# Key sums of a two-layer graph attention kernel: VectorE transposes in place of one TensorE matmul a visit, with the inverses made ahead

## The chip, the cores and the metric

One core of one Trainium2 chip runs the whole program. The metric is the device time in microseconds (us) of one execution, as the median of several. All input, weights and output are float32 in the device's memory; the adjacency is one byte per pair.

## The reference

There are 64 graphs of 256 nodes with 512 features. Two layers follow each other, each of them "normalise the row, clip below zero, attend over the graph's neighbours, add to the input". Layer 0 has 4 heads of 64, layer 1 has 8 heads of 64 with one more normalisation inside and the diagonal always allowed.

```python
h = jnp.maximum(_layernorm(x, axis=-1), 0.0)
x = x + _L0_gnn_ref(h, adj, Wq, Wk, Wv, Wo, bo)
h = jnp.maximum(_layernorm(x, axis=-1), 0.0)
x = x + _L1_gnn_ref(h, adj, gamma, beta, w_qkv, w_out, b_out)
# one attention layer, in short
q, k, v = split_heads(h @ Wq), split_heads(h @ Wk), split_heads(h @ Wv)
sim = jnp.where(mask, einsum('bhid,bhjd->bhij', q, k) * scale, neg)
out = einsum('bhij,bhjd->bhid', softmax(sim, axis=-1), v)
return merge_heads(out) @ Wo + bo
```

The change concerns the softmax's denominator: for every head and query, the sum over the 256 keys of the exponentials, and its inverse, with which the attention's output is multiplied.

## The kernel before

**Tiles and steps.** Two graphs make one step, so there are 32 steps. A step's rows are 4 tiles of 128 nodes by 512 features. Queries, keys and values come from seven matmul products of half-size blocks in place of eight, so a stage such as "project queries and keys" is seven products one after the other (the order `SET`), each of which fills one of four PSUM banks (`mm_tile`, which goes round the four and skips held ones). Two of the seven products are added on to the bank of an earlier one: product 2 goes on to the bank of product 1, and so cannot start until product 1's bank was copied out. In the value projection of layer 1 (`project_v1`, matmuls at L857) it is ScalarE that copies product 1 out, at L750.

**Scores are transposed.** `scores` (L933) leaves keys on the partitions and queries in the free dimension. VectorE adds the mask (L956), ScalarE takes the exponentials in place (L961), GpSimd adds the two key halves (`key_halves`, L968, into `pd`). VectorE transposes `pd` in blocks of 32x32 and sums each block's rows (`turn_keys` L974 and `key_quarters` L981). What is then left, in `part`, is 128 partitions by 32 for each pair of heads: four partition groups of 32, a part of the keys in each. The sum over these four groups is the denominator.

**A visit.** A visit ends one pair of heads' attention and starts another's: `key_sums` of the earlier unit, its weighted values (`weigh_out`, L1004 and the copy L1016), then the scores of the next unit. `key_sums` adds the four groups with one matmul against a 0/1 matrix `quarters` (L1032), inverts (L1036), takes a running maximum for a guard (L1037), writes the inverses to a line in device memory (L1043) and reads each line back, the same for 64 partitions (four DMAs at L1047). `normalise` (L1063, GpSimd) multiplies the attention's output with it. There are 97 calls of `key_sums`: three a step and a few at the edges.

**The order.** The work of every step is a list of events with places, made by hand: `at(period, place, fn)`. A period is 6.4 places long, and in the steady part each holds: `combine` of layer 1 of the step before (place 1.0), a visit at `AT_X` (2.0) with the value projection of layer 1 behind it, `combine` of layer 0 (3.0), queries and keys of layer 1 (3.5), a visit at `AT_Q0` (4.5) with queries and keys of layer 0, values of layer 0 (5.5), a visit at `AT_Z` (6.2). TensorE, VectorE, ScalarE and GpSimd keep the order of this list. SyncE, which issues most DMAs, does not: the build orders its DMAs by when it expects each to be ready, and the order is then fixed in the program.

**DMAs around the visit at `AT_X`.** Here the finished rows of a step leave (`store_graph`, L907, once for each of the two graphs, on SyncE), the inverses are read (L1047), the blocks of the next layer's transposed input are moved with 16 DMAs (`move_blocks`, L711, on SyncE), and the rows of the step after next are read into the buffer that the stores have emptied (`load_graph`, L505, twice, on ScalarE's queue). The two loads stand in ScalarE's own order of instructions, directly ahead of the exponentials of the visit.

```python
at(p, AT_X + 0.005 if s > 1 else 1.2, load_graph, s, 1)
at(p, AT_X + 0.025 if s > 1 else 1.2, load_graph, s, 0)
...
at(p, place + 6 / 7 + 0.001, store_graph, s, 1)
at(p, place + 1.05, store_graph, s, 0)
```

Of the kernel before, what the change touches and what calls it, by code (L numbers as in the profile page):

```python
# [8 lines left out]
FP = mybir.dt.float32  # L9
# [4 lines left out]
ALU = mybir.AluOpType  # L14
# [301 lines left out]
def fast_path(  # L316
# [19 lines left out]
    nc = tc.nc  # L336
    P = 128
# [3 lines left out]
    NSTEP = B // G  # L341
    NIC = N // P
    NT = G * NIC
    T = G * N
# [6 lines left out]
    const = ctx.enter_context(tc.tile_pool(name="const", bufs=1))  # L351
    io = ctx.enter_context(tc.tile_pool(name="io", bufs=2))
    act = ctx.enter_context(tc.tile_pool(name="act", bufs=1))
    sm = ctx.enter_context(tc.tile_pool(name="sm", bufs=2))
    stat = ctx.enter_context(tc.tile_pool(name="stat", bufs=4))
    dram = ctx.enter_context(tc.tile_pool(name="dram", bufs=2, space=bass.MemoryType.DRAM))
# [5 lines left out]
    banks, held = ["m0", "m1", "m2", "m3"], set()  # L362

    def mm_tile(shape, dt=FP, hold=False):
        tag = next(b for b in banks if b not in held)
        banks.remove(tag)
        banks.append(tag)
        if hold:
            held.add(tag)
        return ps_mm.tile(shape, dt, name="mm", tag=tag)  # L370
# [6 lines left out]
        nc.vector.tensor_scalar(offdiag[:, g, :], ident, -1.0, 1.0, op0=ALU.mult, op1=ALU.add)  # L377
    onesb = const.tile([P, P], BF, name="onesb")
    nc.vector.memset(onesb, 1.0)
    quarters = const.tile([P, 32], FP, name="quarters")  # L380
    nc.vector.tensor_tensor(quarters, ident[:, 0:32], ident[:, 32:64], ALU.add)
    for k in (2, 3):
        nc.vector.tensor_tensor(quarters, quarters, ident[:, 32 * k:32 * (k + 1)], ALU.add)
    nc.vector.memset(extremes, 0.0)
    mhalf = const.tile([P, NT], FP, name="mhalf")
    nc.gpsimd.memset(mhalf, -0.5)
# [38 lines left out]
    wqkv1 = const.tile([P, NB, HC, 3, H1], FP, name="wqkv1")  # L425
# [51 lines left out]
    S = [dict() for _ in range(NSTEP)]  # L477
# [433 lines left out]

    units, sums_bank = [0], []

    def scores(s, lyr, pr, second):
        st = S[s]
        qk = st.pop(("qk", lyr, pr))

        sc = [  # L920
            [mm_tile([P, NIC, N]) if second and g == 0 else ps_sc.tile([P, NIC, N], FP, name="sc") for e in range(2)]
            for g in range(G)
        ]
        if second and sums_bank:
            tag = sums_bank.pop()
            banks.remove(tag)
            banks.append(tag)
        for g in range(G):
            for kc in range(NIC):
                for e in range(2):  # L930
                    rows = slice(e * DH, (e + 1) * DH)
                    k0 = g * N + kc * P
                    nc.tensor.matmul(  # L933
                        sc[g][e][:, kc, :], qk[rows, 1, k0:k0 + P],
                        qk[rows, 0, g * N:(g + 1) * N], start=True, stop=True,
                    )

        last = (s, lyr) == (NSTEP - 1, 1)
        if last and pr == 1:
            both = act.tile([P, 2, G, NIC, N], FP, name="p", tag="h")  # L940
            p = [both[:, e] for e in range(2)]
        elif last and pr == 3:
            p = [
                wqk0[:, 4:6].rearrange("p n c k o -> p (n c k o)").rearrange("p (g k n) -> p g k n", g=G, k=NIC),
                act.tile([P, G, NIC, N], FP, name="p", tag="v0"),
            ]
        else:
            p = [sm.tile([P, G, NIC, N], FP, name="p", bufs=4) for _ in range(2)]
        st["sc", lyr, pr], st["p", lyr, pr] = sc, p
# [74 lines left out]
    def key_sums(s, lyr, prs):  # L1024

        st = S[s]
        part = st.pop(("part", lyr, prs))
        rows = 32 * len(prs)
        bank = mm_tile([P, 32])
        sums_bank[:] = [banks[-1]] if len(prs) > 1 else []  # L1030
        sums = bank[:rows]
        nc.tensor.matmul(  # L1032
            sums, part[:, :len(prs)].rearrange("p i b -> p (i b)"), quarters, start=True, stop=True
        )
        inv = stat.tile([P, 32], FP, name="inv", bufs=1)[:rows]
        nc.vector.reciprocal(inv, sums)  # L1036
        nc.vector.tensor_tensor_reduce(  # L1037
            out=sums, in0=sums, in1=inv, scale=1.0, scalar=0.0, op0=ALU.add, op1=ALU.max,
            accum_out=extremes[:rows, units[0]:units[0] + 1],
        )  # L1040
        units[0] += 1
        line = dram.tile([len(prs), 2, T], FP, name="line")
        nc.sync.dma_start(line.rearrange("i e (b q) -> (i e b) q", q=32), inv)  # L1043
        for i, pr in enumerate(prs):
            invb = inverse_place(s, lyr, pr, i if len(prs) > 1 else pr % 2)
            for e in range(2):
                nc.sync.dma_start(  # L1047
                    invb[e * DH:(e + 1) * DH].rearrange("p g n -> p (g n)"),
                    bass.AP(tensor=line.tensor, offset=line[i, e, 0:1].offset, ap=[[0, DH], [1, T]]),
                )  # L1050
            st["invb", lyr, pr] = invb
# [17 lines left out]
    PERIOD, FIRST = 6.4, 6.2  # L1069
# [3 lines left out]
    def at(period, place, fn, *args):  # L1073
        events.append((period * (PERIOD if period >= 0 else FIRST) + place, len(events), fn, args))
# [15 lines left out]
    def visit(period, w, prev, cur):  # L1090

        w -= 0.0003
        s, lyr, prs = prev
        last = (s, lyr) == (NSTEP - 1, 1)
        if prs:
            if prs[0] == 0 and not last:
                at(period, w - 0.0002, place_values, s, lyr)
            at(period, w - 0.0001, key_sums, s, lyr, prs)
            for i, pr in enumerate(prs):
                if not last:  # L1100
                    at(period, w, weigh_out, s, lyr, pr)
                    at(period, w + (0.55 if len(prs) == 1 else (0.3, 0.75)[i]), normalise, s, lyr, pr)
        z, q = w > AT_Z - 0.01 and period < NSTEP - 2, abs(w - AT_Q0) < 0.01 and 0 <= period < NSTEP - 2
        for i, pr in enumerate(cur[2]):
            unit = (*cur[:2], pr)
            one = cur[:2] == (0, 0)
            at(period, w, scores, *unit, i == 1)
            at(period, w, mask_scores, *unit, 0)
            at(period, w + 1 / 7 if one else w, mask_scores, *unit, 1)
            for g, place in enumerate((0.05, 0.22) if one else ((0.02, 0.03), (0.15, 0.3))[i]):  # L1110
                at(period, w + place, exponentials, *unit, g)
            for e, place in enumerate((0.23, 0.3) if one else ((0.1, 0.11), (0.495, 0.496) if z else (0.435, 0.436) if q else (0.35, 0.36))[i]):
                if unit == (1, 0, 1):
                    at(0, 0.45 + place, key_halves, *unit, e)
                else:
                    at(period, w + place, key_halves, *unit, e)
            if cur[:2] == (1, 0):
                period, w, key = 0, 0.0, (*cur[:2], (0, 1), pr)
                turn, add = ((0.44, 0.441), (0.715, 0.87))[pr]
            else:  # L1120
                turn, add = (
                    ((0.31, 0.311), (0.53, 0.531))[pr] if one else ((0.49, 0.491), (0.63, 0.92))[i] if z else
                    ((0.43, 0.431), (1.02, 1.021))[i] if q else ((0.29, 0.291), (0.715, 1.001 if w < AT_X else 0.87))[i]
                )
                key = (*cur, i)
            at(period, w + turn, turn_keys, cur[0])
            at(period, w + add, key_quarters, *key)

    AT_X, AT_C0, AT_QK, AT_Q0, AT_V0, AT_H1, AT_Z = 2.0, 3.0, 3.5, 4.5, 5.5, 6.06, 6.2
# [8 lines left out]
    p = NSTEP - 2  # L1138
# [15 lines left out]
    for s in range(NSTEP):  # L1154

        p = s - 2
# [41 lines left out]
        p = s - 1  # L1198
# [39 lines left out]
        p = s  # L1238
        if s < NSTEP - 1:
# [3 lines left out]
            p, place = (s + 1, 1.0) if s < NSTEP - 2 else (s, LAST_QK + 2)  # L1243
# [5 lines left out]
        else:  # L1249
            p = s - 1  # L1250
# [22 lines left out]
    for i in range(16):  # L1273

        place = (
            *(3.3 - 3.93 + (1 + k) / 7 - 0.0005 for k in range(7)), 0.5205,
            *(0.53 + 0.14 * (k + 1) - 0.0005 for k in range(4)), *(FIRST + 0.9995 for k in range(4)),
        )[i]
        at(-1, place, lambda i=i: weight_block(blocks[i // 4], i // 4, i % 4))
    for i in range(4):  # L1280
        at(-1, 0.1 + 0.01 * i, weight_sum, nc.vector, wqkv1[:, :, :, 0, :], i)
        at(-1, 0.54 + 0.0001 * i, weight_sum, nc.gpsimd, wqkv1[:, :, :, 1, :], i)
        at(0, 0.3, weight_sum, nc.gpsimd, wqkv1[:, :, :, 2, :], i)
        at(0, 1.1, weight_sum, nc.gpsimd, wo1, i)
    for _, _, fn, args in sorted(events, key=lambda e: e[:2]):
        fn(*args)
# [52 lines left out]
```

## Time and profile before

| What | Value |
|---|---|
| Median of 3 runs | 3167.19 us (3165.82 to 3167.96) |
| The profiled execution | 3166.64 us, of which its span is 3164.9 us |
| TensorE (PE) busy | 3136.4 us, 99% of the span |
| GpSimd (POOL) busy | 2237.7 us, 71% |
| VectorE (DVE) busy | 2145.3 us, 68% |
| ScalarE (ACT) busy | 1248.7 us, 39% |
| Mean granted TensorE clock | 0.998 |
| Calls of the key-sum matmul (L1032) | 97, in 194 records |
| SyncE's DMAs of `move_blocks` (L711) | 960 |

A float32 matmul stands in the profile as two records, so the numbers of matmuls in the trace are twice those in the program. Records of TensorE overlap; its pace is read from one start to the next. `SPq` and `ACTq` are the instruction queues of SyncE and ScalarE: a DMA's issue and the wait ahead of it stand there. The arrow behind a gap names what ended it.

### The profile page before, as it was taken

The page shows a single profiled execution, that of the slowest core. Times are in us where ns is not written, and L with a number is a line of the kernel's source. Part 1 is how long each engine was busy: PE and PEld are TensorE (multiplying, and loading weights), DVE is VectorE, ACT ScalarE, POOL GpSimd, SP SyncE. Part 2 cuts the span into 40 slices and gives each one's busy share as a digit, 9 for nine tenths or more (in the row PEclk, how much of TensorE's full clock was granted, in tenths as well). Part 3 has the DMA queues.
Part 4 walks back from the last instruction along what each step waited for, and adds up shares of the span by engine and source line. Part 5 has one row for each costly group of instructions (what it writes and reads, how often), then busy time and mean ns, then how long its engine had stood idle before and what let it go on. Part 6 is the DMA issues. An engine that isn't in the chain of part 4 may idle for free.

```text
span 3164.9 us, 54517 instructions
## 1 busy us (share of the span) xinstructions
PE 3136.4 (99%) x20660; PEld 2582.6 (82%) x20660; DVE 2145.3 (68%) x3590; ACT 1248.7 (39%) x2226; POOL 2237.7 (71%) x2124
## 2 busy tenths in 40 slices
PE   8999999999999999999999999999999999999999
PEld 6788888888888888888888888888888888888887
DVE  6666667666676666666666766667666667666665
ACT  4434444344433444343434434343334434343431
POOL 7776866767767777667677677776776766767753
PEclk9999999999999999999999999999999999999999
DMA  3222222321322322222223223132232222321301
GB/s 127 71 86 71 64 81 70 86 85 51 91 67 78 93 59 74 73 80 86 76 59 90 62 84 87 48 91 70 75 92 64 70 73 79 86 81 52 92 28 48
DMA packets 179851, 237.42 MB, mean 75 GB/s; under 512 B 65272, under 2 KB 69504, under 8 KB 179584
## 3 DMA queue, kind: packets, MB, share of 16 engines
q1 hardware_dynamic: 162832, 202.02, 22.3%
q10 hardware_dynamic: 16752, 31.86, 3.2%
q8 instruction: 165, 2.70, 0.4%
q14 instruction: 102, 0.84, 0.1%
HBM read 136.45 MB, written 34.40 MB: 54 GB/s over the span
## 4 chain that ended last, share of the span: by engine, by line
PE 91%; POOL 3%; DMA 2%; DVE 2%; issue 1%; ACT 0%; SPq 0%; ACTq 0%; POOLq 0%; DVEq 0%
PE mm L816 36%; PE mm L873 17%; PE sc L1004 10%; PE mm L857 10%; PE sc L933 8%; PE mm L843 7%; PE mm L933 2%; DMA out_dram<-xt 1%; POOL xt L511 1%; POOL pd L968 1%; DMA xt<-in_x_dram 1%; PE mm L1032 1%; PE mm L899 0%; POOL oT L1063 0%; DMA h<-in_x_dram 0%
## 5 line engine op out<-in xcount | busy, mean ns | idle before, releaser
L816 PE MATMUL mm<-hT,wqkv 128*128 128x256 f32 x3584 | 787.7, 380 | 0.2 <-DVE qk L756 0.2
L816 PEld LDWEIGHTS mm<-hT,wqkv 128*128 128x128 f32 x3584 | 677.9, 190 | 103.1 <-issue 11.4
L968 POOL TENSOR_TENSOR pd<-p 128x512 f32<-128x512 f32 x383 | 479.4, 1273 | 390.4 <-ACT p L961 250.2
L873 PE MATMUL mm<-wo,oT 128*128 128x256 f32 x2632 | 586.1, 380 | 3.5 <-DVE xt L773 3.2
L873 PEld LDWEIGHTS mm<-wo,oT 128*128 128x128 f32 x2632 | 497.3, 190 | 82.4 <-issue 8.6
L956 DVE TENSOR_TENSOR p<-sc,n 128x512 f32<-128x512 f32 x579 | 363.1, 683 | 271.4 <-PE sc L933 270.0
L961 ACT ACTIVATE p<-p 128x512 f32<-128x512 f32 x766 | 431.8, 624 | 124.7 <-DVE p L956 123.9
L816 PE MATMUL mm<-hT,wqk 128*128 128x256 f32 x1792 | 399.9, 383 | 5.1 <-DVE qk L752 3.7
L857 PE MATMUL mm<-wqkv,hT 128*128 128x256 f32 x1792 | 401.9, 382 | 0.0
L816 PEld LDWEIGHTS mm<-hT,wqk 128*128 128x128 f32 x1792 | 339.0, 191 | 61.5 <-issue 11.8
L857 PEld LDWEIGHTS mm<-wqkv,hT 128*128 128x128 f32 x1792 | 335.5, 190 | 53.4 <-issue 10.3
L1004 PE MATMUL sc<-p,v 128*32 128x256 f32 x6128 | 353.3, 382 | 0.0
L784 POOL TENSOR_TENSOR xt<-xt,u 128x512 f32<-128x512 f32 x183 | 229.9, 1270 | 99.2 <-DVE xt L773 71.6
L933 PE MATMUL sc<-qk 64*128 64x256 f32 x2320 | 292.6, 385 | 0.0
L1004 PEld LDWEIGHTS sc<-p,v 128*32 128x32 f32 x6128 | 190.7, 110 | 119.7 <-issue 2.3
L933 PEld LDWEIGHTS sc<-qk 64*128 64x128 f32 x2320 | 218.7, 186 | 58.4 <-issue 39.2
L974 DVE STREAM_TRANSPOSE turned_p<-pd 128x1024 f32<-128x1024 f32 x192 | 237.1, 1235 | 34.4 <-POOL pd L968 34.4
L1063 POOL TENSOR_TENSOR oT<-oT 128x512 f32<-128x512 f32 x188 | 239.9, 1276 | 3.2 <-DMA oT<-line 3.2
L605 ACT ACTIVATE h<-h,mr,r 128x512 f32<-128x512 f32 x252 | 184.8, 804 | 137.4 <-POOL mr L601 137.4
L981 DVE TENSOR_REDUCE part<-turned_p 128x32 f32<-128x1024 f32 x192 | 233.2, 1215 | 4.4
L843 PE MATMUL mm<-wv,hT 128*128 128x256 f32 x1024 | 227.0, 379 | 0.0
L843 PEld LDWEIGHTS mm<-wv,hT 128*128 128x128 f32 x1024 | 194.2, 190 | 26.7 <-issue 0.3
(141 smaller groups left out, 3738.8 us busy)
## 6 DMA issues: line engine op xcount, KB each, us to landing
h<-blocks SPq DMA_DIRECT2D x960, 64.0 KB, 2.0
oT<-line SPq DMA_DIRECT2D x376, 128.0 KB, 3.3
h<-in_x_dram SPq DMA_DIRECT2D x31, 1024.0 KB, 5.5
out_dram<-xt SPq DMA_DIRECT2D x62, 512.0 KB, 3.6
xt<-in_x_dram ACTq DMA_DIRECT2D x60, 512.0 KB, 5.9
ne<-row SPq DMA_DIRECT2D x30, 256.0 KB, 4.8
ad<-in_adj_dram SPq DMA_DIRECT2D x32, 128.0 KB, 8.5
wr<-in_L_gnn_w_qkv_dram SPq DMA_DIRECT2D x3, 1024.0 KB, 8.9
```

Of the source, the lines that this page charges most:

```text
L816: nc.tensor.matmul(bank[:, k, :], w[:, wa, c, k, a * P:(a + 1) * P], st["hT"][:, ba, c, :], start=first and (k, c) == (0, 0), stop=(k, c) ...
L843: nc.tensor.matmul(bank, st["hT"][:, b0 + t // NIC * step, c % HC, i:i + P], wv0[:, c, :], start=(c == 0), stop=(c == NC - 1),)
L857: nc.tensor.matmul(bank[:, t, :], st["hT"][:, ba, c, t * P:(t + 1) * P], wqkv1[:, wa, c, 2, :], start=first and (t, c) == (0, 0), stop=(t, ...
L873: nc.tensor.matmul(bank[:, t, :], oT[:, ba, c, t * P:(t + 1) * P], w[:, wa, c, :], start=first and (t, c) == (0, 0), stop=(t, c) == (NIC - ...
L933: nc.tensor.matmul(sc[g][e][:, kc, :], qk[rows, 1, k0:k0 + P], qk[rows, 0, g * N:(g + 1) * N], start=True, stop=True,)
L956: nc.vector.tensor_tensor(p[e][:, g], sc[e], neg[:, :, g, :], ALU.add)
L961: nc.scalar.activation(p[e][:, g], p[e][:, g], AF.Exp, scale=SCALE)
L968: nc.gpsimd.tensor_tensor(st["pd"][:, e], p[e][:, :, 0, :], p[e][:, :, 1, :], ALU.add)
L974: nc.vector.transpose(st["turned_p"], st.pop("pd").rearrange("p e g (b k) -> p (e g b) k", k=32))
L981: nc.vector.tensor_reduce(st["part", lyr, prs][:, i], st.pop("turned_p"), axis=mybir.AxisListType.X, op=ALU.add)
L1004: nc.tensor.matmul(po[r0:r0 + 32, g, :], st[f"v{lyr}"][:, g * NIC + kc, pr * P + r0:pr * P + r0 + 32], p[r0 // DH][:, g, kc, :], start=(kc ...
L1063: nc.gpsimd.tensor_tensor(dst, dst, invb, ALU.mult)
```

## The change

Three things change. First, `key_sums` no longer uses TensorE. VectorE transposes the four partition groups of `part` with four transposes of 32 rows into one tile of 32 partitions, sums the four there, and inverts. Second, `key_sums` is split: the sums, the inverse and the write of the line are placed ahead of the visit in the steady periods (`at(*sums, ...)`), and only the reads of the line stay at the visit, as `inverse_in`. Third, four steps near the start move: the last four weight blocks (`weight_block`, 4 transposes on TensorE each) are spread over a projection in place of standing behind it, one set of weight sums on GpSimd (`weight_sum` of `wqkv1[..., 2, :]`) goes from place 0.3 to 0.65, and one `turn_keys` of step 1 goes from 0.53 to 0.6583. The matrix `quarters` and the bank that the sums took are gone.

```diff
-    units, sums_bank = [0], []
+    units = [0]
...
-        if second and sums_bank:
-            tag = sums_bank.pop()
-            banks.remove(tag)
-            banks.append(tag)
...
     def key_sums(s, lyr, prs):
 
         st = S[s]
-        part = st.pop(("part", lyr, prs))
-        rows = 32 * len(prs)
-        bank = mm_tile([P, 32])
-        sums_bank[:] = [banks[-1]] if len(prs) > 1 else []
-        sums = bank[:rows]
-        nc.tensor.matmul(
-            sums, part[:, :len(prs)].rearrange("p i b -> p (i b)"), quarters, start=True, stop=True
-        )
-        inv = stat.tile([P, 32], FP, name="inv", bufs=1)[:rows]
+        part = st.pop(("part", lyr, prs))[:, :len(prs)].rearrange("p i b -> p (i b)")
+        nb = 32 * len(prs)
+        keys = sm.tile([P, 7, 2 * 32], FP, name="keys", tag="turned_p", bufs=1)[:32, :, :nb]
+        for k in range(4):
+            nc.vector.transpose(keys[:, k], part[32 * k:32 * (k + 1)])
+        sums, inv, both = (keys[:, k] for k in (4, 5, 6))
+        nc.vector.tensor_reduce(
+            sums, keys[:, :4].rearrange("b k q -> b q k"), axis=mybir.AxisListType.X, op=ALU.add
+        )
         nc.vector.reciprocal(inv, sums)
...
-        line = dram.tile([len(prs), 2, T], FP, name="line")
-        nc.sync.dma_start(line.rearrange("i e (b q) -> (i e b) q", q=32), inv)
+        line = st["line", lyr, prs] = dram.tile([len(prs), 2, T], FP, name="line")
+        nc.sync.dma_start(
+            line.rearrange("i e (b q) -> (e b) i q", q=32), inv.rearrange("b (i q) -> b i q", q=32)
+        )
+
+    def inverse_in(s, lyr, prs):
+
+        st = S[s]
+        line = st.pop(("line", lyr, prs))
         for i, pr in enumerate(prs):
...
-            at(period, w - 0.0001, key_sums, s, lyr, prs)
+            if (s, lyr) == (1, 0):
+                sums = 0, 0.88
+            elif 0 <= period < NSTEP - 2 and s > 0:
+                sums = (
+                    (period, AT_X + 1.45) if abs(w - AT_Q0) < 0.01 else
+                    (period, AT_Q0 + 1.022) if abs(w - AT_Z) < 0.01 else (period - 1, AT_Z + 1.25)
+                )
+            else:
+                sums = period, w - 0.0001
+            at(*sums, key_sums, s, lyr, prs)
+            at(period, w - 0.00008, inverse_in, s, lyr, prs)
...
-                    ((0.31, 0.311), (0.53, 0.531))[pr] if one else ((0.49, 0.491), (0.63, 0.92))[i] if z else
+                    ((0.31, 0.311), (0.6583, 0.6585))[pr] if one else ((0.49, 0.491), (0.63, 0.92))[i] if z else
...
-            *(0.53 + 0.14 * (k + 1) - 0.0005 for k in range(4)), *(FIRST + 0.9995 for k in range(4)),
+            *(0.53 + 0.14 * (k + 1) - 0.0005 for k in range(4)), *(FIRST + (2 + k) / 7 - 0.0005 for k in range(4)),
...
-        at(0, 0.3, weight_sum, nc.gpsimd, wqkv1[:, :, :, 2, :], i)
+        at(0, 0.65, weight_sum, nc.gpsimd, wqkv1[:, :, :, 2, :], i)
```

More of the change, by code (lines that the diff above doesn't have):

```diff
@@ L379, in fast_path @@
     nc.vector.memset(onesb, 1.0)
[L380 to L383, printed above, removed]
     nc.vector.memset(extremes, 0.0)
@@ L1026, in key_sums @@
         st = S[s]
-        part = st.pop(("part", lyr, prs))
-        rows = 32 * len(prs)
-        bank = mm_tile([P, 32])
-        sums_bank[:] = [banks[-1]] if len(prs) > 1 else []
-        sums = bank[:rows]
-        nc.tensor.matmul(
-            sums, part[:, :len(prs)].rearrange("p i b -> p (i b)"), quarters, start=True, stop=True
+        part = st.pop(("part", lyr, prs))[:, :len(prs)].rearrange("p i b -> p (i b)")
[6 more added lines that the diff above has]
+            sums, keys[:, :4].rearrange("b k q -> b q k"), axis=mybir.AxisListType.X, op=ALU.add
         )
-        inv = stat.tile([P, 32], FP, name="inv", bufs=1)[:rows]
         nc.vector.reciprocal(inv, sums)
         nc.vector.tensor_tensor_reduce(
-            out=sums, in0=sums, in1=inv, scale=1.0, scalar=0.0, op0=ALU.add, op1=ALU.max,
-            accum_out=extremes[:rows, units[0]:units[0] + 1],
+            out=both, in0=sums, in1=inv, scale=1.0, scalar=0.0, op0=ALU.add, op1=ALU.max,
+            accum_out=extremes[:32, units[0]:units[0] + 1],
         )
         units[0] += 1
-        line = dram.tile([len(prs), 2, T], FP, name="line")
-        nc.sync.dma_start(line.rearrange("i e (b q) -> (i e b) q", q=32), inv)
+        line = st["line", lyr, prs] = dram.tile([len(prs), 2, T], FP, name="line")
[5 more added lines that the diff above has]
+        line = st.pop(("line", lyr, prs))
         for i, pr in enumerate(prs):
```

## The prediction

> **What bounds the kernel now.** The page comes first: TensorE is busy for 99% of the span at almost full clock, and the chain that ended last is TensorE for 91%.
>
> ```profile
> PE 3136.4 (99%) x20660; PEld 2582.6 (82%) x20660; DVE 2145.3 (68%) x3590; ACT 1248.7 (39%) x2226; POOL 2237.7 (71%) x2124
> PE 91%; POOL 3%; DMA 2%; DVE 2%; issue 1%; ACT 0%; SPq 0%; ACTq 0%; POOLq 0%; DVEq 0%
> ```
>
> So what TensorE no longer does is won, and what makes it wait is lost. Next is the timeline of TensorE around the visit at `AT_X` in a steady period (start, us, what).
>
> ```profile
> 1279.29 0.30 PE L1032 MATMUL mm<-quarters,part 128*64 128x32 f32 x2
> 1279.52 3.66 PE L1004 MATMUL sc<-p,v 128*32 128x256 f32 x64
> ...
> 1286.77 7.17 PE L857 MATMUL mm<-wqkv,hT 128*128 128x256 f32 x32
> ```
>
> The key-sum matmul takes 1279.29 to 1279.52. The values of layer 1 (L857) start at 1286.77. Then the timelines of SyncE and of ScalarE at the same place:
>
> ```profile
> 1279.73 0.38 SPq L907 DMA_DIRECT2D out_dram<-xt  x1
> 1280.37 0.48 SPq L1043 DMA_DIRECT2D line<-inv  x1
> 1281.48 0.38 SPq L907 DMA_DIRECT2D out_dram<-xt  x1
> 1282.97 2.37 SPq L1047 DMA_DIRECT2D oT<-line  x4
> 1285.44 12.28 SPq L711 DMA_DIRECT2D h<-blocks  x16
> ```
>
> ```profile
> 1283.25 0.58 ACT L1016 COPY oT<-sc 128x512 f32<-128x512 f32 x1 [1.14 <-PE sc L1004]
> 1284.34 0.37 ACTq L505 DMA_DIRECT2D xt<-in_x_dram  x1
> 1285.06 1.23 ACT L961 ACTIVATE p<-p 128x512 f32<-128x512 f32 x2 [1.23 <-DVE p L956]
> ...
> 1288.80 0.58 ACT L750 COPY v<-mm 128x512 f32<-128x512 f32 x1 [1.37 <-PE mm L857]
> ```
>
> SyncE stores both graphs before it reads the inverses back and before its 16 moves. ScalarE's load of new rows (L505) goes into the buffer that these stores empty; it starts 2.86 us after the second store's issue, and the exponentials (L961) stand behind it. That ScalarE waits in line for the store shows in the listing of that line, where one wait lasted 3.37 us:
>
> ```profile
> L505 ACTq EVENT_SEMAPHORE  x58: 17/28/3368, 109.5 to 2938.2; - x58
> ```
>
> Last, the start, where TensorE does stand:
>
> ```profile
> 25.75 1.97 PE L816 MATMUL mm<-hT,wqk 128*128 128x256 f32 x8 [1.16 <-DVE qk L756]
> 51.54 3.64 PE L816 MATMUL mm<-hT,wqk 128*128 128x256 f32 x8 [3.71 <-DVE qk L752]
> 105.33 0.66 PE L469 MATMUL mm<-ident,wr 128*128 128x128 f32 x4 [3.33 <-DVE qk L760]
> 107.84 1.12 PE L469 MATMUL mm<-ident,wr 128*128 128x128 f32 x4 [1.86 <-DVE qk L762]
> 109.24 5.46 PE L1004 MATMUL sc<-p,v 128*32 128x256 f32 x64
> ```
>
> Eight records take 1.97 us after a wait of 1.16 and 3.64 us after one of 3.71; L1004 takes 5.46 in place of 3.66 after the next pair. So a long stand costs some 1.8 us more, because the clock then runs at half for about 3.4 us.
>
> **The change part by part.** The sum is made against the profiled execution's 3166.64 us, 0.55 under the median. I keep the old line numbers.
>
> *The matmul goes.* 97 x 0.23 us (1279.29 to 1279.52, the same at the other two visits) = 22.3 us, all on the path. The switch to 32-column weights stays: from L873 to L1032 it takes 309 ns from start to start, and once, without a key sum, from L857 to L1004 also 309. The bank that the sums held is freed; nothing waits for it.
>
> *Key sums on VectorE.* Before, one cost 0.34 + 0.19 + 0.13 = 0.67 us. A 64-column transpose is not in the trace. By the rows of 1024 columns (1235 ns) and 512 (683 ns) it is some 200 ns, so four cost 0.8; the sum over 256 elements lies between 258 ns (100 elements) and 1215 (1024), say 0.42; the inverse of 64 columns takes 0.34 to 0.69 by the row of 32. That is 1.9 to 2.4 us, 1.2 to 1.7 more a call. It is placed where VectorE has room: at 1243.7 it stood idle for 4.04 us, and at 1305 for 2.83 before L752. At 1269.3 the gaps behind are 0.17, 0.96, 1.03, 1.03 and 1.03, so a delay of 2.1 us is caught up within three products of `combine`. I cost it at nothing; uncovered, it would be 97 x 1.4 = 136 us. At the 10 or so edge calls that are not moved, the matmul's wait goes and the work comes: nothing net.
>
> *The order on SyncE.* This decides. As built, the changed program has in each of 29 periods: line, store of one graph, four reads of the line (L1047), 16 moves (L711), and only then the store of the other graph (L907). Since the line is now written early, its reads are ready before the second store, and the moves went along with them. ScalarE's order is unchanged in these periods: its first load still waits for both stores and stands ahead of four exponentials and the copy L750. Step by step, from 1279.29:
> - The store of the first graph is issued at 1279.73 as before. The reads follow once the last product of `combine` is done, at 1280.2, and take 2.47 us (1282.97 to 1285.44): 1282.7. The transposes that feed the moves end about then too.
> - The 16 moves took 12.28 us here, 10.26 in the set behind the next visit, and 10.03 to 14.32 over all 60 sets. The long ones share the DMA engines with the new rows, which now come later, so I take 10.5: 1293.2.
> - A store lands in 3.6 us (median, 2.8 to 5.3): 1296.8. Before, ScalarE was let go at 1284.34.
> - ScalarE then issues its load (0.37), makes four exponentials (2.17 for four in a later visit) and copies product 1 out (0.58): 1299.9.
> - TensorE needs that copy for product 2. It starts L857 at 1286.54 (0.23 earlier) and has done three products of 8 records, at 216 ns each, at 1291.7. It stands for 8.2 us.
> - The half clock behind adds 1.8, as above.
> - GpSimd's key halves follow the exponentials and its sums for `combine` of layer 0 follow those: I take 0.8 us more (0 if VectorE's backlog hides it, 1.5 if each of the 10 or so instructions runs on the late edge).
>
> This gives 10.8 us a period, 29 x 10.8 = 313 us. Lower bound: moves 10.03, landing 2.8, GpSimd 0, so 8.7 a period. Upper: moves 12.9 (the common length at this visit), landing 4.5, GpSimd 1.5, so 14.8.
>
> A rule of the Trainium skill speaks to this. The row: 16 issues fill SyncE's queue for 10.03 us or more, while one such move lands in 2.0 us by the page. "DMA: Bandwidth & Descriptors", section "Issuing engines are not separate DMA queues", says that issuing from several engines saves only the sequencer's issue time, which is usually small beside the DMA itself. By that rule the store would lose a few tenths of a microsecond behind the moves and the result would be the matmul's gain; the row says that here issue is the larger part, and I go by the row.
>
> *The start.* The first wait (3.71 + 1.8 = 5.5 us) goes, since L752 no longer stands behind L974, which waited for GpSimd. The second (3.33 + 1.86 + 1.8 = 7.0) goes too, but what is late next is GpSimd: from 87.16 to past 131 it is busy almost without a gap, and VectorE's L974 at 122.71, with L754 behind it in line, waits for it whatever TensorE does. So the second gain is given back at product 3 of L857, and of the first I count 5 us. Bounds: 0 and 12.5.
>
> Sum: 3166.6 - 22.3 - 5 + 313 = 3452.5, and 3453 with the 0.55.
>
> **The rivals.**
> - *The store does not hold TensorE up; only the matmul's gain is left.* 3167.2 - 22.3 - 5 = 3140 (3130 to 3146), faster. It decides for this if ScalarE is let go by 1288.6 (1291.7 less 3.1): the moves would have to pass in 2.3 us in place of 10. For it: TensorE has no wait on ScalarE beyond 0.2 us today. Against it: no set of moves took less than 10.03.
> - *Key sums on the path.* The added VectorE time is exposed at each call: 3167.2 - 27 + 136 = 3276, slower. For it: TensorE already waits 0.2 to 1.0 us for L773 in `combine` of layer 0, at the place of one of the new calls. Against it: the gaps above.
> - *The full hold-up.* Moves stay at 12.9, landing is 4.5 and the GpSimd chain adds 1.5 or more: 3167 - 22 + 29 x 14.8 = 3574.
> - That the matmul stays after all is ruled out: the order of the changed program has no L1032 on TensorE.
>
> **How the numbers follow.** Main case 0.79 (3385 to 3540), full hold-up 0.10, store without effect 0.07, key sums exposed 0.03, all cancelling 0.01. The low end is 3167 - 35 + 29 x 8.7 = 3384. From the upper end I leave out the rare joint case, so 3385 to 3545. A change within 0.2% (6 us, about what measurement of this kernel can tell) has 0.01, faster 0.07, slower 0.92.
>
> **What would show it.** Right: L857 with a gap of 7 to 11 us released by ScalarE's L750, 29 times, eight records at half clock behind each; L505's wait at 10 us or more; L907 in SyncE's timeline behind 16 L711; no L1032; the key sums' VectorE instructions at 1.9 to 2.4 us with no TensorE wait on them. Wrong: the second store lands before the exponentials are due, or TensorE's new waits name VectorE or GpSimd first.

## The result and the profile after

The changed kernel takes 3498.85 us (median of 4 runs, 3495.74 to 3499.74), the kernel before 3166.79 on the same chip: a ratio of 1.1047, 95% interval 1.1027 to 1.1066. The profiled execution took 3499.74 us, with a span of 3498.0 and a mean granted clock of 0.958 in place of 0.998. New line numbers of what matters: L1035 writes the line, L1046 reads it, L903 stores a graph, L707 moves blocks, L501 loads rows, L953 exponentials, L746 the copy of product 1, L853 values of layer 1, L869 `combine`, L996 the visit's first matmuls, L507 the bias that GpSimd adds to new rows, L1062 `normalise`.

The page's busy times and its chain:

```profile
PE 3187.0 (91%) x20466; PEld 2604.2 (74%) x20466; DVE 2322.0 (66%) x4072; ACT 1240.8 (35%) x2226; POOL 2240.3 (64%) x2124
PE 69%; POOL 9%; SPq 8%; DMA 5%; issue 4%; DVE 2%; ACT 1%; ACTq 1%; POOLq 0%; DVEq 0%
```

TensorE's share of the chain fell from 91% to 69%, and SyncE's queue, nothing before, has 8%. TensorE's timeline at a visit at `AT_X`, near the time of the one in the prediction, shows where:

```profile
1300.72 5.45 PE L853 MATMUL mm<-wqkv,hT 128*128 128x256 f32 x24
1314.61 3.78 PE L853 MATMUL mm<-wqkv,hT 128*128 128x256 f32 x8 [8.44 <-ACT v L746]
1318.18 1.06 PE L558 MATMUL mm<-identb,adb 128*128 128x128 bf16 x8
```

Before, 32 records of the values ran without a gap in 7.17 us. Now the last 8 of them wait 8.44 us for ScalarE's copy, take 3.78 us in place of 1.97, and the eight behind them 1.06 in place of 0.61; the granted clock was 0.50 over both of these rows. SyncE's timeline tells why:

```profile
1282.22 0.38 SPq L527 DMA_DIRECT2D row<-any_of  x1
...
1290.60 0.34 SPq L532 DMA_DIRECT2D ne<-row  x1
1291.05 0.37 SPq L1035 DMA_DIRECT2D line<-keys  x1
1293.93 0.38 SPq L903 DMA_DIRECT2D out_dram<-xt  x1
1295.83 2.37 SPq L1046 DMA_DIRECT2D oT<-line  x4
1298.30 10.03 SPq L707 DMA_DIRECT2D h<-blocks  x16
1308.43 0.53 SPq L903 DMA_DIRECT2D out_dram<-xt  x1
```

Before, both stores (L907) stood ahead of the reads. Now the second ("the store" from here on) is issued at 1308.43, right behind 10.03 us of moves. ScalarE's timeline continues from there:

```profile
1297.21 0.59 ACT L1008 COPY oT<-sc 128x512 f32<-128x512 f32 x1 [1.14 <-PE sc L996]
1311.42 0.37 ACTq L501 DMA_DIRECT2D xt<-in_x_dram  x1
1311.90 0.63 ACT L953 ACTIVATE p<-p 128x512 f32<-128x512 f32 x1 [14.11 <-DMA out_dram<-xt]
...
1313.99 0.56 ACT L746 COPY v<-mm 128x512 f32<-128x512 f32 x1
```

The load goes out 2.99 us after the store, once that has landed; the first exponential, a compute instruction that needs nothing of the load, stands behind it in ScalarE's order, and ScalarE stood idle for 14.11 us before it. The same in every period, from the waits (engine, line, waited for: us in all, times, longest; the last line is of the kernel before):

```profile
PE mm L853 <- ACT v L746: 270.5, 29, 11.5
PE mm L869 <- DVE xt L769: 13.4, 22, 0.7
PE mm L869 <- POOL oT L411: 4.5, 11, 1.1
```

```profile
ACT p L953 <- DMA out_dram<-xt: 434.9, 29, 17.1
```

```profile
PE mm L873 <- DVE xt L773: 3.2, 8, 0.7
```

The key sums themselves, on VectorE ahead of the visit, cost what was estimated, and no wait of TensorE names them:

```profile
1283.50 0.96 DVE L1023 STREAM_TRANSPOSE keys<-part 32x64 f32<-32x64 f32 x4
1284.50 0.58 DVE L1025 TENSOR_REDUCE keys<-keys 32x64 f32<-32x256 f32 x1
1285.11 0.54 DVE L1028 RECIPROCAL keys<-keys 32x64 f32<-32x64 f32 x1
```

That `combine` waits for VectorE's L769 for 13.4 us in place of 3.2 comes with the late store and not with them: run 4 below keeps the key-sum matmul, has the store even later, and waits 13.3 us at that place.

**Where the time went.** By the trace, a period grew from 97.27 to 108.89 us on average, 11.6 more. Taken from the start of one of TensorE's stages to the start of the next, the stall is 9.5 (9.70, less one record's 0.22), the half clock 2.25 (1.80 in the eight records behind the stall, 0.22 in the eight of L558, 0.24 in the 24 behind those), `combine` of layer 0 takes 0.6 more (6.99 in place of 6.41), and three key-sum matmuls give back 0.7. Every other stage takes the same time as before to 0.01 us. Over 29 periods the 11.6 are 337 us; the start gives back 3.3 (TensorE reaches the projection behind the first `combine` at 134.41 in place of 137.72) and the ten other matmuls 2.3. The 331 of this sum stands beside a span that grew by 333.1; some 2 us are not assigned.

### The profile page after: what moved, and what is told of

It reads as the page before. It is cut to its first block, busy times and chain, and to the rows that moved or that the text cites. A ratio compares the mean times of both kernels' runs of the same rounds, so it can differ in the third digit from the quotient of the medians.

```text
span 3498.0 us, 54547 instructions
## 1 busy us (share of the span) xinstructions
PE 3187.0 (91%) x20466; PEld 2604.2 (74%) x20466; DVE 2322.0 (66%) x4072; ACT 1240.8 (35%) x2226; POOL 2240.3 (64%) x2124
## 4 chain that ended last, share of the span: by engine, by line
PE 69%; POOL 9%; SPq 8%; DMA 5%; issue 4%; DVE 2%; ACT 1%; ACTq 1%; POOLq 0%; DVEq 0%
PE mm L812 31%; PE mm L869 11%; PE sc L996 9%; SPq L707 8%; PE mm L839 6%; PE sc L925 6%; PE mm L853 3%; DMA out_dram<-xt 2%; POOL pd L960 2%; POOL xt L507 2%; POOL oT L1062 2%; PE mm L925 2%; DMA row<-any_of 1%; DMA line<-keys 1%; DVE p L948 1%
## 5 line engine op out<-in xcount | busy, mean ns | idle before, releaser
L853 PE MATMUL mm<-wqkv,hT 128*128 128x256 f32 x1792 | 466.1, 420 | 272.3 <-ACT v L746 270.5
L853 PEld LDWEIGHTS mm<-wqkv,hT 128*128 128x128 f32 x1792 | 370.1, 211 | 349.1 <-ACT v L746 282.1
L953 ACT ACTIVATE p<-p 128x512 f32<-128x512 f32 x766 | 430.5, 623 | 499.8 <-DMA out_dram<-xt 434.9
L869 PE MATMUL mm<-wo,oT 128*128 128x256 f32 x2632 | 590.1, 381 | 18.6 <-DVE xt L769 13.4
L869 PEld LDWEIGHTS mm<-wo,oT 128*128 128x128 f32 x2632 | 495.9, 190 | 102.9 <-POOL n L569 24.2
L996 PE MATMUL sc<-p,v 128*32 128x256 f32 x6128 | 351.4, 381 | 0.0
L996 PEld LDWEIGHTS sc<-p,v 128*32 128x32 f32 x6128 | 189.7, 110 | 146.0 <-issue 31.2
L748 DVE TENSOR_TENSOR v<-mm,v 128x512 f32<-128x512 f32 x32 | 22.1, 692 | 363.1 <-ACT v L746 358.6
L780 POOL TENSOR_TENSOR xt<-xt,u 128x512 f32<-128x512 f32 x183 | 230.6, 1274 | 30.8 <-DVE xt L776 13.5
L1062 POOL TENSOR_TENSOR oT<-oT 128x512 f32<-128x512 f32 x188 | 240.5, 1279 | 0.0
```

What stands on the lines that cost most here:

```text
L853: nc.tensor.matmul(bank[:, t, :], st["hT"][:, ba, c, t * P:(t + 1) * P], wqkv1[:, wa, c, 2, :], start=first and (t, c) == (0, 0), stop=(t, ...
L869: nc.tensor.matmul(bank[:, t, :], oT[:, ba, c, t * P:(t + 1) * P], w[:, wa, c, :], start=first and (t, c) == (0, 0), stop=(t, c) == (NIC - ...
L953: nc.scalar.activation(p[e][:, g], p[e][:, g], AF.Exp, scale=SCALE)
L996: nc.tensor.matmul(po[r0:r0 + 32, g, :], st[f"v{lyr}"][:, g * NIC + kc, pr * P + r0:pr * P + r0 + 32], p[r0 // DH][:, g, kc, :], start=(kc ...
L1062: nc.gpsimd.tensor_tensor(dst, dst, invb, ALU.mult)
```

## The experiments

My theory: the cause is one order on SyncE (the second store behind 16 moves) and one order on ScalarE (a load that waits for that store, ahead of exponentials and a copy that TensorE needs). The rivals: the key sums on VectorE cost the time, or the traffic and the late moves do. Twelve kernels were run, on three chips. The kernel before took 3174, 3175 and 3183 us on them, so ratios are compared, and microseconds only within one group of four.

All times "behind the visit" below count from the first matmul of the visit at `AT_X` (the key-sum matmul where there is one), as means over 29 periods. Of the kernel before there is a profile of the first chip only. Run 8, with the same order in the steady periods, shows on its own chip a period of 97.49 us in place of 97.27, the load 4.3 us behind the store in place of 3.9, the exponentials at 7.0 in place of 6.6, and `combine` of layer 0 waiting 8.2 us in all in place of 3.2. So differences of this size to the kernel before may be the chip's.

**1. The store ahead of the moves** (`store_first`)

```diff
-            at(p, place + 1.05, store_graph, s, 0)
+            at(p, place + 0.9995, store_graph, s, 0)
```

> The second graph's store is listed before the visit instead of behind it; as built, SyncE then issues it after one read of the line and ahead of the 16 moves. Everything else is the changed kernel. Theory (the late store holds ScalarE's load, and with it the exponentials and the copy that TensorE needs): the 9.5 us wait of TensorE on ScalarE's copy L746 is gone in all 29 periods, and so is the half clock behind it; what is left is the matmul's gain and the start, 3499 - 29 x 12.3 = 3142 us (3135 to 3155), under the kernel before. Rival 1 (key sums on VectorE are what costs): nothing changes, 3490 to 3500. Rival 2 (only the place where TensorE waits moves, because the reads of the inverses or the moves are late for something else): 3200 to 3400, with a new wait on VectorE or GpSimd in each period.

Measured: 3183.69 us, ratio 1.0031 (1.0021 to 1.0042). This one store is worth 0.10 of the ratio: the wait on L746 is gone in all periods. But the theory's number was missed by 35 us (the kernel before took 3174 here, so 3149 was due), and the waits name most of it, 34.6 us in place of 3.2:

```profile
PE mm L869 <- DVE xt L769: 18.9, 30, 0.7
PE mm L869 <- POOL oT L411: 15.7, 23, 1.6
```

The store now leaves 3.9 us behind the visit, since one read of the line is still ahead of it; before it left at 2.2. The exponentials start at 8.3 in place of 6.6, GpSimd's sums follow them, and `combine` of layer 0 waits for those. The small follow-up that the prediction priced at 0.8 us a period is 1.1 here ((34.6 - 3.2) / 29), without any long stall ahead of it.

**2. The key sums at the visit again, still on VectorE** (`sums_at_visit`)

```diff
-            elif 0 <= period < NSTEP - 2 and s > 0:
+            elif False:
```

> The key sums stay on VectorE, but none is made ahead: all stand directly before their visit, as in the kernel before. The list of the stores is untouched; as built, SyncE then has both stores ahead of the line and its reads again, with one move before the reads and 15 behind. Theory (the early line is what let the moves pass the second store): the 9.5 us wait goes, 3140 to 3150 us if the 2.3 us of VectorE work at each visit is covered. Rival (key sums on the path decide): 97 x up to 2.3 us come in at the visits, 3167 - 22 + 136 to 223 = 3280 to 3370. Rival 2 (moving the sums has no part in it): about 3499.

Measured: 3247.56 us, ratio 1.0226 (1.0213 to 1.0239). The 9.5 us stall is gone here too, so making the inverses ahead is indeed what let the moves pass the store. The work is not covered at the visit, though: 73 us over the kernel before, between the theory's number and the rival's. The line is written later, its reads begin 7.0 us behind the visit in place of 4.6, and GpSimd, which had no such wait to speak of, waits for them in `normalise`, ahead of the sums for `combine`:

```profile
POOL oT L1062 <- DMA oT<-line: 66.3, 23, 3.8
```

VectorE's work itself also shows: the last scores of the visit wait for its mask additions, which stand behind the key sums, and take 0.8 us more in each period (4.44 in place of 3.65), 23 us of the loss. So the second part of the change is needed for the first. It also brought the loss.

**3. Only ScalarE's order changed** (`loads_late`)

```diff
-            at(p, AT_X + 0.005 if s > 1 else 1.2, load_graph, s, 1)
-            at(p, AT_X + 0.025 if s > 1 else 1.2, load_graph, s, 0)
+            at(p, AT_X + 0.32 if s > 1 else 1.2, load_graph, s, 1)
+            at(p, AT_X + 0.321 if s > 1 else 1.2, load_graph, s, 0)
```

> SyncE's order and everything else as in the changed kernel, with the second store still behind the 16 moves; only the two loads of new rows stand in ScalarE's order behind the eight exponentials and the copy L746, ahead of the copy of the adjacency L563. Theory (the store costs only because ScalarE waits for it in line, ahead of what TensorE needs): the wait of TensorE on L746 goes although the store is as late as ever, and the load is ready at about the time it is reached; 3140 us plus at most 2 us a period at L563, so 3140 to 3200. Rival (the DMA traffic or the late moves themselves are what costs): 3400 to 3500.

Measured: 3509.45 us, ratio 1.1053 (1.1037 to 1.1069), about the rival's number. Its reason is not the rival's. TensorE's wait on L746 is gone, as the theory had it, and the exponentials start at 5.5 in every period. The wait has moved one engine on, to GpSimd, which adds the bias to the new rows in line ahead of the sums that `combine` needs:

```profile
PE mm L869 <- POOL oT L411: 221.2, 29, 8.1
PE mm L869 <- issue: 60.9, 29, 3.4
```

```profile
POOL xt L507 <- DMA xt<-in_x_dram: 358.0, 29, 13.6
```

I had looked at ScalarE's order alone and had not followed the loaded rows to their first user. A late store costs nearly the same whichever of the two engines stands in line for it.

**4. The kernel before with the store behind the moves** (`before_store_last`): SyncE (`EngineType.SP`) joins the engines whose order is the hand-made list. This puts the store behind the moves, and the line behind the read of the neighbour row.

```diff
-    ctx.enter_context(tc.manual_schedule(engines={... EngineType.Pool}))
+    ctx.enter_context(tc.manual_schedule(engines={... EngineType.Pool, mybir.EngineType.SP}))
```

> The kernel before, with its matmul and its inverses at the visit, but SyncE keeps the order of the hand-made list as the other engines do; the second store then stands behind the reads and the 16 moves. Theory (the order on SyncE alone makes the loss): TensorE waits on ScalarE's copy L750 in 29 periods here too. The moves start 7.5 us after the last product of combine and take about 10.3, the landing 3.0, load, exponentials and copy 3.1, so the copy is done at 24 us where it is due at about 13: 11 us of stall, 2.3 of half clock and 0.6 behind, 29 x 13.9 = 402, so 3569 us (3530 to 3640). Rival (the new key sums are part of the loss): clearly less than the 3499 of the changed kernel, 3167 to 3300.

Measured: 3599.77 us, ratio 1.1340 (1.1323 to 1.1356): with the matmul and the inverses where they were, the loss is larger than the changed kernel's. The reads come later here (5.8 behind the visit in place of 2.8), so the stall is 12.1 us in place of 9.5, and the matmul's 22 us are not won.

```profile
PE mm L857 <- ACT v L750: 346.5, 29, 13.3
```

The first and this run settle the cause from both sides: put the store ahead and the changed kernel is rid of nearly all of its loss; put it behind and the kernel before gets one.

**5. Both stores ahead of the reads, by the list** (`sp_listed_store_first`): the edits of 1 and 4 on the changed kernel.

> Two edits: SyncE keeps the order of the hand-made list, and the second graph's store is listed ahead of the visit. In each period SyncE then has line, store of one graph, read of the neighbour row, store of the other graph, four reads of the line, 16 moves. In the run with the store ahead of the moves but behind one read of the line (3184 us against 3174 of the kernel before) that read waited for the line until 3.8 us after the visit's first matmul, so the exponentials came 3.1 us later than in the kernel before (8.6 against 5.5 us behind the visit's first matmul), GpSimd's sums came as much later, and combine of layer 0 waited 1.4 us a period. Theory: with no read ahead of it the store goes at 2.2 us, the exponentials start at 5.5 as before, the waits of combine (35 us in all) go, and the matmul's 22 us and the start's 3 are left: 25 us under the kernel before on the same chip (ratio 0.990 to 0.994), L869's waits on GpSimd and VectorE under 8 us. Rival (the 35 us come from the key sums on VectorE, which hold up what combine needs): the waits stay, and the ratio is 1.000 to 1.004.

Measured: 3172.59 us, ratio 0.9993 (0.9984 to 1.0002). Better than run 1, as expected, but the gain of 25 us did not come. The store left at 2.2 as planned, but the load could go only 5.3 us after it (3.9 in the kernel before, 3.0 where the store stands behind the moves). The four reads follow it at 2.8 behind the visit, where the kernel before reads at 4.6. The exponentials start at 8.0, and `combine` waits 26.6 us in all. (The 5.5 that the expectation gives for the kernel before was read off one period; its mean is 6.6.) That the reads slow the landing fits these numbers, but was not tried by itself, and the neighbour row, issued 1.3 us ahead of the store, is as good a candidate.

**6. The second store on ScalarE's queue** (`store_on_act`), the rest as changed:

```diff
-        nc.sync.dma_start(
+        (nc.sync if g else nc.scalar).dma_start(
...
-            at(p, place + 1.05, store_graph, s, 0)
+            at(p, place + 0.9995, store_graph, s, 0)
```

> The changed kernel, with the second graph's store issued from ScalarE's queue, ahead of its two copies of the visit, in place of SyncE's. SyncE's order is otherwise that of the changed kernel: line behind the row read, reads as late as there, then 16 moves. Theory (the place behind the moves in SyncE's queue is the cause, not the memory traffic, the reads or the key sums): the store is issued 2.2 us behind the visit's first matmul, the load of new rows at about 5.2, the exponentials at 5.6, and the 9.5 us stall and the later waits go: 20 to 26 us under the kernel before (ratio 0.991 to 0.995). Rival (the reads that wait for the late line hold normalise on GpSimd too): 3 us a period at combine of layer 0, ratio 1.01 to 1.03.

Measured: 3158.68 us, ratio 0.9951 (0.9938 to 0.9965): faster than both kernels, and at the edge of the theory's range; the load left at 6.6 us on average in place of 5.2. SyncE's order is that of the changed kernel, with row read (L532), line, first store, reads and moves one after the other, only without the second store:

```profile
1174.83 0.34 SPq L532 DMA_DIRECT2D ne<-row  x1
1175.26 0.38 SPq L1035 DMA_DIRECT2D line<-keys  x1
1177.59 0.38 SPq L903 DMA_DIRECT2D out_dram<-xt  x1
1181.18 2.37 SPq L1046 DMA_DIRECT2D oT<-line  x4
1183.64 11.87 SPq L707 DMA_DIRECT2D h<-blocks  x16
```

```profile
1179.33 0.39 ACTq L903 DMA_DIRECT2D out_dram<-xt  x1
...
1184.60 0.37 ACTq L501 DMA_DIRECT2D xt<-in_x_dram  x1
```

An issue of 0.39 us on another queue turns a ratio of 1.105 into 0.995. That leaves the place in the queue as the cause; moves, reads and key sums are all still there. The gain is 16 us (11 to 20) of the 26 that the matmul (22.3) and the start (3.3 as measured) give. `combine`'s waits, 14.6 us against 3.2 in the kernel before and 8.2 in run 8 on this chip, are 6 to 11 us of what is missing.

**7. Line ahead of the row read, store still late** (`sp_listed`): the edit of 4 on the changed kernel.

> The changed kernel with SyncE in the order of the hand-made list: line and one store ahead of the read of the neighbour row, then the reads, the 16 moves and the second store, as late as in the changed kernel. It tests one term: in the changed kernel the reads began 3.1 us after the last matmul of combine began (I had put 1.1), by my reading because the line stands in SyncE's queue behind the row read, which waits for a landing. Theory: the line goes out 5 us earlier, the reads begin 1 to 2 us earlier, and so do moves, store and copy; 29 x 1 to 2 = 29 to 58 us under the changed kernel's ratio of 1.105, so 1.086 to 1.096. Rival (the reads wait for something else, their buffer or the end of combine): 1.103 to 1.107.

Measured: 3476.94 us, ratio 1.0950 (1.0934 to 1.0967). The reads begin 1.1 us earlier (1.7 behind the visit, 2.8 in the changed kernel), the moves 0.9, and a period is 0.8 shorter. The ratio lies at the near end of the theory's range. So the line's place behind the row read was a little over half of what the prediction missed there; what is left (1.7 against 0.9 predicted) is here the row read itself, which the list puts directly ahead of the reads.

**8. The start steps alone** (`start_only`), on the kernel before.

> The kernel before with only the three steps near the start moved (the last four weight blocks, one set of weight sums on GpSimd, one transpose of the key quarters of step 1). Theory: the two stands at 51.5 and 105 us go (5.5 and 7.0 us with their half clock), most of it is given back to GpSimd and VectorE behind; in the changed kernel TensorE reached the projection behind the first combine 3.3 us earlier, so 2 to 5 us under the kernel before (ratio 0.9985 to 0.9993). Rival (the stands only move): within 1 us.

Measured: 3170.20 us, ratio 0.9983 (0.9974 to 0.9992), so 3 to 8 us where 2 to 5 were expected; TensorE leaves the first `combine` 2.9 us earlier than in the kernel before.

**9 to 12. Is more to be had, and are the key sums free?** The first moves the loads of run 6 behind the first four exponentials (`AT_X + 0.1`), the second does so to run 1, the third to run 8 (key sums still a matmul). The fourth is the first with the transposes and the sum of each key sum done twice:

```diff
+        for _ in range(2):
+            [nc.vector.transpose(keys[:, k], part[32 * k:32 * (k + 1)]) for k in range(4)]
+            nc.vector.tensor_reduce(
...
```

> The version with the second store on ScalarE's queue (ratio 0.995), and the two loads of new rows placed behind the first four exponentials instead of ahead of and between them. There, the store landed 3.1 to 5.9 us after its issue, so the exponentials began 5.7 to 8.5 us behind the visit's first matmul in place of 5.5, and combine of layer 0 still waited 14.6 us in all. Theory (what was left is still ScalarE waiting in line for a landing, handed on by GpSimd): the exponentials begin at 5.5 in every period, GpSimd's key halves at 7.4 to 7.5, the loads at 7.8 to 8.1, and L869's waits fall to under 4 us. Then the matmul's 22 us and the start's 3 to 5 are left: 3147 to 3151 us beside 3174.8, ratio 0.990 to 0.993. Rival (combine's waits come from the key sums on VectorE): L869's waits stay at 12 to 15 us, ratio 0.994 to 0.996.

> The version with the second store on SyncE ahead of the moves but behind one read of the line (ratio 1.003), with the loads behind the first four exponentials. There the store left 3.9 us behind the visit's first matmul and landed 3.9 us later, the exponentials began at 8.2 on average, and combine waited 35 us. Theory: the exponentials begin at 5.5; the load follows at 7.8 to 9.3, new rows land some 3 us later, and GpSimd, which adds the bias to them at about 11.2, waits up to 1 us in some periods: ratio 0.991 to 0.996. Rival (the line's reads and the moves are what costs, wherever ScalarE's loads stand): 1.000 to 1.004.

> The kernel before with the three start steps and with the loads behind the first four exponentials; the key sums stay one matmul a visit, and the inverses are made at the visit. Theory: SyncE stores both graphs early here already, so the loads' place is worth only the few waits of combine (8 us in the run with the start steps alone): ratio 0.995 to 0.998, and the distance of the first kernel of this call to this one is the matmul alone, 97 x 0.23 = 22 us. Rival (the loads' place is the gain and the matmul's removal is worth nothing): within 5 us of the first kernel of this call.

> The first kernel of this call with the four transposes and the sum of each key sum done twice: 0.96 + 0.58 = 1.54 us more on VectorE at each of 97 calls, 149 us in all. Theory (the key sums lie in VectorE's gaps): at most a tenth of it is seen, ratio up to 0.004 above that kernel. Rival (VectorE's added work is on the path in part, the prediction's second rival): 50 to 149 us more, ratio 0.016 to 0.047 above.

| Kernel | us | Ratio to before (95%) | Exponentials start | L869's waits, us |
|---|---|---|---|---|
| before | 3183.37 | 1 | 6.6 | 3.2 |
| `store_act_loads_mid` | 3165.27 | 0.9939 (0.9925 to 0.9952) | 5.5 | 21.9 |
| `store_first_loads_mid` | 3183.11 | 0.9997 (0.9988 to 1.0006) | 5.5 | 38.8 |
| `start_loads_mid` | 3194.04 | 1.0031 (1.0019 to 1.0043) | 5.8 | 28.2 |
| `sums_twice` | 3179.95 | 0.9988 (0.9978 to 0.9997) | 5.5 | 27.7 |

(The last two columns of "before" are from its profile on the first chip.) The three expectations on the place of the loads failed in the same way: the exponentials start on time, but L869's waits did not fall. The second kernel's ratio is 0.003 under run 1's all the same, though its period is not shorter (98.02 us against 97.93): a difference of this size between ratios of two chips is not to be read as a gain. The loads leave later (8.6 us behind the visit in the first, 6.6 in run 6), and GpSimd now waits for the rows, as in run 3:

```profile
POOL xt L507 <- DMA xt<-in_x_dram: 24.2, 12, 2.8
```

So the chain that is left is store, landing, load, landing, bias; reordering ScalarE only chooses which engine stands for it. The first kernel and run 6 can't be told apart (their intervals overlap) and share the place of the fastest version. Between the first and the third the difference is 28.8 us on one chip, where the rival had at most 5: 22.3 of the matmul and 6.3 of L869's waits fit it, though the two also differ in the store's queue and in the place of the key sums. The matmul's gain is real where nothing else is made late. `sums_twice` put 149 us more on VectorE and lost 14.7, a ratio of 0.005 above the first kernel: about the theory's 0.004, and far from the rival's 0.016. The small loss hides a larger one. `combine` of layer 1 takes 13.07 us in place of 12.18, 26 us over 29 periods, and `combine` of layer 0 6.59 in place of 7.19, 17 us less; the other 6 us of the loss lie outside the steady periods. With the sums made once, `combine` of layer 1 takes 12.18 us as in the kernel before: one set of key sums lies in VectorE's gaps, a second one does not wholly.

## Why the prediction was right

The range of 3385 to 3545 held 3498.85, on the forecast side and by the forecast mechanism: L853 stands for L746 29 times, with eight records at half clock behind, L903 behind 16 L707, no key-sum matmul, and key sums of 2.36 us (1.9 to 2.4 predicted) that no matmul waits for. One announced sign did not appear where I put it: the load's own wait is 5.4 us at most in the listing of its line; the profile charges ScalarE's long wait to the exponential behind it (434.9 us, above).

The forecast was 46 us short, in these terms of the sum (times from the visit's first matmul):

| Step | Predicted | Measured (mean) |
|---|---|---|
| reads begin | 0.9 | 2.81 |
| reads to moves | 2.5 | 2.64 |
| 16 moves | 10.5 | 10.26 |
| store to load | 3.6 | 3.03 |
| load to end of copy | 3.1 | 3.1 |
| stall of TensorE | 8.2 | 9.5 |
| half clock | 1.8 | 2.25 |
| later waits | 0.8 | 0.6 |

- **Mis-sized: "The reads follow once the last product of `combine` is done, at 1280.2".** I took the early line for landed by then. It was inverted at 1285.65, but stood on SyncE behind the read of the neighbour row, which waited for a landing of its own until 1290.60; it went out at 1291.05 and the reads 4.78 us later. What ended their wait is the line's landing: in the 18 periods in which the trace tells it, the line landed 4.7 us after its issue on average (1.4 in the median of all 97 lines), and the reads followed 0.1 us later. Of this step I had not asked what was queued ahead of it. That is 1.9 us a period; the shorter landing took 0.6 of it back. Run 7 showed a little over half of it to be the line's place.
- **Mis-sized: the half clock.** I counted the eight records behind the wait; the eight of L558 behind them run slow as well (1.06 in place of 0.61 here), and in some periods the next values do: 2.25 us on average in place of 1.8.
- **The start** gave 3.3 us in place of 5, within its 0 to 12.5, and run 8 by itself 3 to 8.
- **The matmul**, 0.23 us at each of 97 calls, held: from the visit's first matmul to L853 it is 7.25 us in place of 7.48, and the switch of tile shape from `combine` to L996 takes 309 ns as it did to L1032.
- **The rivals.** "The store does not hold TensorE up" needed ScalarE free early; it was let go 18.8 us behind the visit. "Key sums on the path" (3276) fell with runs 6 and 12, but it is in part what run 2 shows once they stand at the visit. "The full hold-up" did not come in the changed kernel, whose moves took 10.26 us and not 12.9; run 4 has a longer stall, 12.1 us, but from later reads, with moves of 10.2 us and a landing of 3.0.
- **The rule weighed against the row.** By "DMA: Bandwidth & Descriptors" of the Trainium skill, section "Issuing engines are not separate DMA queues", a store on another engine saves only issue time, usually small beside the transfer. Here the issue time ahead of it was 10.03 us for 16 moves, each of which lands in 2.0 us, and run 6 showed what another queue saves: from a ratio of 1.105 to 0.995. Run 1 got most of that on SyncE's own queue (1.003), so it is the 16 issues ahead of the store that cost.

## What to carry to other kernels

Before making a DMA's data ready earlier, list what its queue holds behind it: an early transfer takes followers along, and a store or load that was harmless in second place may now stand behind a long row of issues. For each DMA that an engine issues in its own order, follow both ends: what computes behind it on that engine while it waits, and who first uses what it brings. And price a step by the landing that its neighbour in the queue waits for, not only by its own data.

## What the runs showed of the hardware

- Sixteen issues on SyncE took 10.03 us at the least when no rows were on the way (10.26 on average in the changed kernel), and 11.6 to 13.5 on average in the kernels whose loads run beside them (13.0 before; run 2, which has the four reads among its moves, is left out).
- The same store let the load behind it go after 3.0 us when it stood behind the moves, 3.9 in the kernel before, 4.4 from ScalarE's queue (run 6), and 5.3 with a neighbour row issued 1.3 us ahead of it and four line reads right behind it.
- After a stand of 8.4 us TensorE ran at half speed over 8 float32 records and part of 8 bf16 ones (3.78 and 1.06 us in place of 1.97 and 0.61, at a granted clock of 0.50); the mean granted clock fell to 0.958, and to 0.946 with the longer stands of run 4.
- The kernel before took 3167, 3174, 3175 and 3183 us on four chips: 0.5%, more than several of the differences measured here, which is why only ratios on one chip are compared. In the steady periods of run 8 all of the difference to the first chip lies in `combine` of layer 0 (6.62 us a period in place of 6.41); every other stage takes the same time to 0.01 us.
